# Batch 1 transposed on TensorE, and a work order planned anew with other transfer and clock costs

## The chip, the cores and the metric

The kernel runs on one core of one Trainium2 chip, in a single launch. The metric is the device time of a whole execution in microseconds. Every matrix product runs on TensorE (PE in the profile; its weight loads are PEld). VectorE is DVE, ScalarE is ACT, GpSimd is POOL. All transfers are issued by one queue, SyncE's (SP, SPq where its queue is meant), and carried by the core's 16 DMA engines.

## The reference

Eight batches of x (512 rows x 256) attend to a context (512 x 512 per batch), and then go through a mixture of 16 experts, of which each row uses 8, plus one shared expert. Cut to what matters:

```python
# attention
src_trans = (einsum('bsf,of->bso', ctx, W_src) + b_src) * mask      # keys and values
tgt_trans = (einsum('btf,of->bto', layernorm(x), W_tgt) + b_tgt) * mask
attn = softmax(where(mask == 0, -inf, q @ k / sqrt(32)))            # 8 heads of 32
x = x + concat(layernorm(x), attn @ v) @ W_out + b_out
# mixture of experts on layernorm(x)
scores = sigmoid(l2norm(xf) @ l2norm(gate_w).T)                     # 16 experts, top 8
routed = sum over experts of combine * ((silu(xf @ w_gate) * (xf @ w_up)) @ w_down)
x = x + routed + silu(xf @ sw_gate) * (xf @ sw_up) @ sw_down
```

## The kernel before

Each float32 operand of a product is split into two float16 halves, a high one and a low one, and each product is three TensorE matmuls (`mm3`: low by high, high by low, high by high). The split costs one ScalarE instruction for the high half and one subtract, on VectorE or GpSimd, for the low one.

A matmul sums over the partitions, so x, the attention output and the routed input have to be transposed. The kernel has two ways. For batch 0, TensorE multiplies by the identity into PSUM (tiles xT, oT, fT), and `split` reads PSUM: ScalarE writes the high half, VectorE the low one. For batches 1 to 7, `turn` splits the natural rows in SBUF first (tiles xm, om, fm of the pool `c16`), and two DMA transposes per `turn` bring 32 blocks each into xh, oh and f. In xm and om the low half is made by GpSimd, in fm by VectorE. The context goes the same way (cn to ch, 64 blocks a transfer), and so do the attention weights (pn to pt, 128 blocks a transfer, 128 of them in all).

Attention works in units: a batch has eight (two groups of four heads by four row blocks). A unit writes its scores s into the only score buffer (S=1, four PSUM banks), VectorE takes the row maximum nm, ScalarE scales it and computes four exponentials p. Two pairs of p are then rounded on ScalarE (pn high), subtracted on GpSimd (pn low, 128x1024), transposed by DMA into pt, and multiplied by v on TensorE (tile o). The scores of the next unit can only be written when the four p have read those before.

The experts (`ffn`) run over 17 weight sets in four groups, with the products g and u (up to 512 columns) and y. The weights arrive as float32 (tiles raw) during the setup, and are split on ScalarE and VectorE into w.

No engine order is written by hand. `record` lists operations, each with an engine, an assumed duration, and a virtual time `vt` to which a table RANK adds an offset by kind of operation and by batch (-1 setup, 0, 1, 7, and 2 for the batches between). `schedule` simulates engines and buffers, and picks among operations within AHEAD of the oldest pending virtual time the one that can start first, ties by virtual time. The resulting order is the order of the instructions; each engine keeps it and waits on semaphores. SLOTS gives the number of buffers of each pool: `row` holds q32, the float32 query between its product and its split (two per batch), and in the setup gw_n, the gate weights; `oc` holds a unit's output.

At run time, the planner's costs have no influence beyond the order and the buffer that they chose. In the trace every recorded instruction has the same line (L1071, the call in the last loop), so groups are told apart by their tile names.

Of the kernel before, what the change touches and what calls it, by code (L numbers as in the profile page):

```python
# [9 lines left out]
F32 = mybir.dt.float32  # L10
# [9 lines left out]
P = 128  # L20
# [11 lines left out]
    x=2, n2=5, cx=4, c16=2, ch=1, xh=1, f=2, qk=4, row=2, mb=1, mx=2, mt=1, p32=2, pn=2, pp=3, v3=2, oc=2, oh=2,  # L32
# [98 lines left out]
class Plan:  # L131
# [5 lines left out]
    def add(self, eng, dur, calls, port=False, size=0, after=()):  # L137
        outs, ins = [], list(after)
        for _, out, args, kw in calls:
            outs += [o for o in (*out, kw.get("accum_out")) if is_view(o)]  # L140
            ins += [a for a in (*args, *(v for k, v in kw.items() if k != "accum_out")) if is_view(a)]
        name = (outs[0] if isinstance(outs[0], Buf) else outs[0].buf).name
        tag = "".join(c for c in name if not c.isdigit()).strip("_") + eng
        vt = self.vt + RANK.get(tag, {}).get(STAGE.get(self.batch, 2), 0.0)
        op = Op(eng, dur, calls, outs, ins, vt, len(self.ops), port, size)
        op.tag = (self.batch, tag)
        self.ops.append(op)
        return op
# [31 lines left out]
    def dve(self, n, meth, out, *args, **kw):  # L180
        calls = [self.call("vector." + meth, out, *args, **kw)]
        self.add("DVE", 150 + 1.04 * n + 66 * (meth == "scalar_tensor_tensor" and any(is_view(a) for a in args[1:2])), calls, port=self.shared(calls))
# [11 lines left out]
    def dmat(self, tiles, out, in_):  # L194
        self.add("SP", max(1240.0, 16.4 * tiles), [self.call("sync.dma_start_transpose", out, in_)], size=4000 * tiles)

    def dma(self, size, out, in_):
        self.add("SP", 360.0, [self.call("sync.dma_start", out, in_)], size=size)


AHEAD = 1.366
RANK = {
    "aACT": {0: 0.1537, 1: 0.0033, 2: -0.4983, 7: 0.1955},
    "aDVE": {0: 0.0254, 1: 0.2498, 2: -0.2428},
    "aPOOL": {0: -0.0113, 1: 0.6968, 2: 0.5586, 7: 0.0013},
    "amaPE": {-1: 0.2806},
    "ambPE": {-1: 0.1166},
    "bobDVE": {-1: 0.5078},
    "bobSP": {-1: -0.2061},
    "bvbDVE": {-1: 0.105},  # L210
    "cTPE": {0: 0.5508},
    "cbSP": {0: 0.2177, 2: 0.7056, 7: 0.5622},
    "cdSP": {0: 0.0041, 1: -0.029, 2: 0.2104},
    "chACT": {0: -0.6068},
    "chDVE": {0: 0.2153},
    "chSP": {1: 0.0075, 2: -0.8976, 7: -1.0876},
    "cnACT": {1: -0.6307, 2: -0.7293, 7: -0.9914},
    "cnDVE": {1: 0.0087, 2: -0.0023, 7: 0.0346},
    "colsSP": {-1: -0.0672},
    "csBPE": {2: -0.1535, 7: -0.0124},  # L220
    "csTPE": {0: -0.1204, 1: -0.0287, 2: -1.2814, 7: -0.0309},
    "ctACT": {0: 0.864, 1: 0.1003, 2: 0.7227, 7: -0.1018},
    "cxPOOL": {0: 0.6459},
    "cxSP": {-1: 0.0735, 1: 0.0526, 2: -0.9286, 7: -0.0609},
    "fACT": {0: 0.0039},
    "fDVE": {0: 1.0851},
    "fSP": {1: 0.3396, 2: -0.0242, 7: 0.4824},
    "fTPE": {0: 0.3035},
    "fmACT": {1: 0.3782, 2: -0.0974, 7: -0.0187},
    "fmDVE": {2: 0.5311, 7: -0.0959},  # L230
    "fmPE": {-1: -0.1267},
    "fmaPE": {-1: 0.1564},
    "fmbPE": {-1: -0.4319},
    "gPE": {0: 0.1235, 1: 0.207, 2: 0.1559, 7: 0.6056},
    "gTPE": {0: 0.3676, 1: 0.5965, 2: -0.1162, 7: -0.0034},
    "gsqDVE": {-1: -0.4317},
    "gw_nDVE": {-1: -0.1543},
    "gw_nSP": {-1: -2.0117},
    "gwsACT": {-1: 0.0234},
    "gwsDVE": {-1: 0.6316},  # L240
    "hACT": {0: -0.6213, 1: 0.3291, 2: -0.1853, 7: -0.0131},
    "hDVE": {0: 0.1408, 1: 0.0071, 2: -0.2515, 7: -0.0144},
    "hPOOL": {0: -0.3695, 1: 0.2141, 2: -0.0944, 7: 0.3346},
    "junkACT": {1: -0.0113, 2: -0.018, 7: 0.0007},
    "kACT": {0: 0.3565, 1: -0.9183, 2: -0.1216},
    "kDVE": {0: 0.4038, 1: 0.1818, 2: -0.0333, 7: 0.0991},
    "kPE": {0: -0.2174, 1: -0.0614, 2: -0.0344, 7: -1.3012},
    "lgPE": {0: 0.2761, 1: -0.3919, 2: -0.2135, 7: 0.0154},
    "mbSP": {-1: -0.7576, 1: 0.96, 2: 0.035, 7: 0.1462},
    "mcolDVE": {-1: -0.5544},  # L250
    "mkSP": {-1: -0.0456},
    "mkTPE": {-1: -0.2494},
    "mrDVE": {0: 0.88, 1: 0.1094, 2: 0.5668},
    "mvDVE": {0: 0.3115, 1: 0.2223, 2: 0.1576, 7: -0.6709},
    "mwDVE": {1: -0.5933, 2: 0.5831, 7: -0.1328},
    "nmACT": {0: 0.3158, 1: -0.251, 2: -0.0551, 7: -0.0427},
    "nmDVE": {0: 0.0026, 1: 0.0593, 2: -0.1259, 7: -0.1155},
    "oPE": {0: 0.0273, 1: -0.0232, 2: 0.0553, 7: 0.0423},
    "oTPE": {0: 0.1833},
    "ocACT": {0: 0.1024, 1: 0.1925, 2: 0.2005, 7: 0.4061},  # L260
    "ocDVE": {0: 0.1704, 1: -0.1219, 2: -0.6326, 7: -0.0917},
    "ohACT": {0: 0.4072},
    "ohDVE": {0: -0.1733},
    "ohSP": {1: 0.1129, 2: -0.0398, 7: -0.3174},
    "omACT": {2: 0.2922, 7: 0.0002},
    "omPOOL": {1: -0.0603, 2: -0.0508, 7: 0.7467},
    "onPOOL": {0: 0.7499, 1: -0.853, 2: -0.1829, 7: -0.2491},
    "onesPOOL": {-1: -0.3119},
    "ooPE": {0: 0.4931, 1: -0.4365, 2: -0.6844, 7: -0.4352},
    "outSP": {0: 0.4027, 1: -0.3028, 2: 0.4122, 7: 0.4538},  # L270
    "pACT": {0: 0.0182, 1: -0.6748, 2: -0.0234},
    "pnACT": {0: 0.2152, 1: 0.2561, 2: 0.1906, 7: 0.0196},
    "pnPOOL": {0: 0.1635, 1: 0.0141, 2: 0.2234},
    "ptSP": {0: 0.4655, 1: -0.4384, 2: 0.1266, 7: 0.3368},
    "qACT": {0: 0.1257, 1: -0.3375, 2: -0.3996, 7: -0.129},
    "qDVE": {0: -0.2704, 1: -0.4202, 2: -0.5367, 7: -0.2649},
    "qPE": {0: -0.3731, 1: -0.0506, 2: -0.194, 7: -1.1345},
    "qPOOL": {0: -0.0185, 1: 0.126, 7: -0.8731},
    "rDVE": {0: -0.1233, 1: -0.1058, 2: 0.0001, 7: -0.3334},
    "rawSP": {-1: -0.1474},  # L280
    "rhPOOL": {0: -0.1646, 1: -0.4627, 2: 0.6826, 7: 0.2987},
    "riDVE": {0: -0.198, 1: 0.6361, 2: 0.1284, 7: -0.0834},
    "sPE": {1: 0.0314, 2: -0.3686, 7: -0.8384},
    "scACT": {0: -0.0831, 1: 0.4518, 2: -0.1934, 7: -0.1498},
    "scDVE": {0: 0.3459, 1: -0.1583, 2: 0.1869, 7: -0.186},
    "scPOOL": {0: -0.0709, 1: 0.1093, 2: -0.1766, 7: 0.0205},
    "smallDVE": {-1: 0.3026, 1: -0.1537, 2: -0.254, 7: -0.5587},
    "smallPOOL": {-1: -0.2347, 0: -0.1282, 1: -0.3163, 2: 0.0089, 7: 0.0576},
    "sqwACT": {-1: -0.5218},
    "sqwPOOL": {-1: -0.1816},  # L290
    "tDVE": {0: 0.0006, 1: -0.5031, 2: 0.36, 7: 0.0922},
    "uDVE": {0: 0.1229, 1: 0.634, 2: -0.239, 7: -0.259},
    "uPE": {0: -0.1486, 1: 0.6035, 2: 0.715},
    "vACT": {0: 0.2058, 1: 0.1873, 2: -0.0086, 7: 0.1161},
    "vDVE": {0: 0.3577, 1: 0.1322, 2: -0.9791, 7: -0.0565},
    "vPE": {0: 1.1408, 1: -1.3367, 2: -0.1245, 7: 0.2457},
    "vPOOL": {0: -0.0824, 1: -0.3013, 2: -0.4353, 7: 0.59},
    "veDVE": {0: 0.124, 1: -0.0703, 2: -0.0253, 7: -1.3962},
    "vfDVE": {0: 0.0546, 1: -0.7051, 2: 0.0069, 7: 0.2438},
    "wACT": {-1: -0.1553},  # L300
    "wDVE": {-1: -0.0168},
    "wmaPE": {-1: -0.2382},
    "wmbPE": {-1: -0.7302},
    "woACT": {-1: -0.6539},
    "woDVE": {-1: 0.1164},
    "woTPE": {-1: 0.5609},
    "wo_nSP": {-1: 0.2082},
    "wsACT": {-1: -0.3273},
    "wsDVE": {-1: -0.0925},
    "wsTPE": {-1: 0.9299},  # L310
    "ws_naSP": {-1: -0.9149},
    "ws_nbSP": {-1: 0.0231},
    "wtACT": {-1: 0.4585},
    "wtDVE": {-1: 0.4299},
    "wtTPE": {-1: -0.4778},
    "wt_nSP": {-1: 0.0823},
    "xDVE": {0: 0.124, 1: 0.2257, 2: -0.3319, 7: 0.1379},
    "xPOOL": {0: -0.0121, 1: 0.02, 2: 0.1123, 7: -0.199},
    "xSP": {0: 1.1008, 1: 0.0058, 2: 0.0641, 7: 0.353},
    "xTPE": {0: 0.4516},  # L320
    "xfACT": {0: -0.1806, 1: 0.1451, 2: -0.1422, 7: -0.437},
    "xhDVE": {0: 0.6081},
    "xhSP": {1: 0.2024, 2: -0.7682, 7: 0.2589},
    "xmACT": {1: 0.1813, 2: 0.1954},
    "xmPOOL": {1: -0.0234, 2: 0.0256, 7: 0.0077},
    "xnACT": {0: 0.0363, 1: -0.1228, 2: 0.2161, 7: -0.0338},
    "xnSP": {-1: -4.4201, 1: -0.3353, 2: -0.0611, 7: -0.0009},
    "xoPE": {0: -0.2204, 1: -0.0378, 2: -0.3262, 7: -0.1335},
    "yPE": {0: 0.3541, 2: 0.148, 7: 0.1762},
# [772 lines left out]
```

## Time and profile before

| quantity | value |
|---|---|
| median of 3 runs (lowest, highest) | 963.44 us (959.19, 963.85) |
| profiled execution, its own time | 962.42 us |
| its span, first to last instruction | 960.3 us |
| PE busy / DVE / ACT / POOL | 860.6 / 668.5 / 654.2 / 680.4 us |
| mean granted TensorE clock | 0.972 of full |
| transfers | 152.43 MB in 395,542 packets |
| PE busy in 0 to 300 us, in 300 to 860 us | 227.79 us, 537.46 us |

A busy share is time with an instruction of that engine running. "Idle before" a group names the operation that ended the wait. PEclk is the clock that TensorE was granted. A window line has the busy time of PE, PEld, DVE, ACT and POOL in that stretch, the granted clock, the mean share of the DMA engines and their rate.

### The profile page before, as it was taken

The numbers are of one execution on the slowest core, as the hardware profiler recorded it, in microseconds if no ns is written. First come the engines' busy times: TensorE is split into PE (matmuls) and PEld (weight loads), VectorE is DVE, ScalarE is ACT, GpSimd is POOL, SyncE is SP. The second block draws the span as 40 slices with busy tenths as digits, with TensorE's granted clock in tenths as the row PEclk, the third lists the DMA queues.
The fourth block names the chain that finished last, engine by engine and source line by source line (L and its number), as shares of the span: only waits on it lengthen the run. The fifth ranks groups of instructions, "written<-read, shape, count | busy, mean of one in ns | idle before, by whom it ended". The sixth has DMA issues, their size and how long they took to land.

```text
span 960.3 us, 21139 instructions
## 1 busy us (share of the span) xinstructions
PE 860.6 (90%) x8007; PEld 547.0 (57%) x8007; DVE 668.5 (70%) x1311; ACT 654.2 (68%) x1133; POOL 680.4 (71%) x830
## 2 busy tenths in 40 slices
PE   3874768989789998989999999989999999999997
PEld 2452446766555565636655556646555666565655
DVE  6666778855876677757785688757886687567554
ACT  3588887874877687757786587757787777534231
POOL 4577778876768787677858786787848976853432
PEclk9886999999889999999999999999999999999999
DMA  8868787798699967999599977998499968951411
GB/s 254 271 124 175 138 157 130 151 197 162 121 205 184 201 133 139 211 191 178 104 198 182 197 145 137 204 191 181 88 189 197 178 110 144 214 120 26 123 56 44
DMA packets 395542, 152.43 MB, mean 159 GB/s; under 512 B 347008, under 2 KB 375216, under 8 KB 395440
## 3 DMA queue, kind: packets, MB, share of 16 engines
q1 hardware_dynamic: 395440, 151.08, 77.9%
q8 instruction: 63, 1.03, 0.5%
q14 instruction: 39, 0.32, 0.2%
HBM read 61.12 MB, written 4.46 MB: 68 GB/s over the span
## 4 chain that ended last, share of the span: by engine, by line
PE 55%; DMA 12%; ACT 11%; DVE 8%; POOL 5%; issue 3%; SPq 1%; POOLq 0%; ACTq 0%; DVEq 0%
PE y L1071 14%; PE u L1071 13%; PE g L1071 12%; DMA pt<-pn 8%; PE s L1071 4%; ACT p L1071 3%; PE o L1071 3%; POOL pn L1071 3%; PE v L1071 3%; DVE nm L1071 3%; PE k L1071 2%; ACT pn L1071 2%; DMA cb<-cd 2%; PE oo L1071 2%; SPq L1071 1%
## 5 line engine op out<-in xcount | busy, mean ns | idle before, releaser
L1071 POOL TENSOR_TENSOR pn<-p,pn 128x1024 f16<-128x1024 f32 x128 | 274.6, 2151 | 57.8 <-ACT pn L1071 48.7
L1071 PEld LDWEIGHTS <-w 128*128 128x128 f16 x1836 | 172.1, 98 | 172.1 <-issue 19.3
L1071 POOL TENSOR_TENSOR a<-a,cb 128x512 f32<-128x512 f32 (+1 forms) x144 | 166.1, 1165 | 73.5 <-DVE a L1071 34.6
L1071 ACT ACTIVATE p<-s,nm,small 128x512 f32<-128x512 f32 x256 | 192.3, 782 | 10.6 <-POOL pn L1071 8.1
L1071 PE MATMUL g<-f,w 128*128 128x512 f16 (+1 forms) x918 | 194.7, 357 | 3.7 <-DVE oc L1071 1.3
L1071 PE MATMUL u<-f,w 128*128 128x512 f16 (+1 forms) x918 | 194.1, 358 | 1.6 <-DVE a L1071 1.6
L1071 PE MATMUL y<-w,h 128*128 128x256 f16 x1632 | 185.9, 273 | 5.6 <-DVE h L1071 4.1
L1071 PEld LDWEIGHTS <-h 128*128 128x128 f16 x1632 | 158.5, 98 | 32.0 <-DVE h L1071 6.7
L1071 ACT CAST pn<-p 128x1024 f16<-128x1024 f32 x128 | 134.5, 1053 | 60.8 <-DMA pt<-pn 60.7
L1071 DVE TENSOR_REDUCE nm<-s 128x4 f32<-128x2048 f32 x64 | 146.2, 2285 | 14.7 <-PE s L1071 14.6
L1071 ACT ACTIVATE a<-g,small 128x512 f32<-128x512 f32 (+1 forms) x153 | 98.1, 645 | 51.7 <-PE g L1071 49.8
L1071 DVE SCALAR_TENSOR_TENSOR a<-a,g 128x512 f32<-128x512 f32 (+1 forms) x153 | 94.5, 622 | 39.1 <-ACT a L1071 38.0
L1071 ACT CAST h<-u 128x512 f16<-128x512 f32 (+1 forms) x117 | 62.8, 540 | 51.0 <-DVE u L1071 49.2
L1071 PEld LDWEIGHTS <-pt 128*128 128x128 f16 x2048 | 69.8, 97 | 36.8 <-DMA pt<-pn 16.5
L1071 DVE TENSOR_TENSOR h<-u,h 128x512 f16<-128x512 f32 (+1 forms) x117 | 72.6, 625 | 25.7 <-ACT h L1071 24.1
L1071 DVE SCALAR_TENSOR_TENSOR x<-y,small,x 128x512 f32<-128x512 f32 x64 | 47.8, 748 | 60.9 <-PE y L1071 60.6
L1071 DVE TENSOR_TENSOR u<-u,a 128x512 f32<-128x512 f32 (+1 forms) x108 | 68.4, 635 | 27.5 <-PE u L1071 22.7
L1071 PE MATMUL o<-v,pt 128*128 128x65 f16 (+1 forms) x2048 | 74.2, 187 | 13.5 <-DMA pt<-pn 10.9
L1071 PE MATMUL s<-k,q 32*128 32x512 f16 x768 | 56.1, 396 | 21.2 <-ACT p L1071 20.7
L1071 POOL TENSOR_TENSOR on<-oc,r 128x128 f32<-128x128 f32 x64 | 30.1, 472 | 31.9 <-DVE oc L1071 20.1
L1071 POOL TENSOR_TENSOR h<-a,h 128x512 f16<-128x512 f32 (+1 forms) x36 | 40.3, 1120 | 15.2 <-ACT h L1071 14.9
L1071 PE MATMUL k<-ch,ws 128*128 128x512 f16 x192 | 45.6, 390 | 5.4 <-DMA ch<-cn 4.1
(188 smaller groups left out, 1055.8 us busy)
## 6 DMA issues: line engine op xcount, KB each, us to landing
cb<-cd SPq DMA_DIRECT2D x112, 256.0 KB, 3.9
cx<-in_ctx_dram SPq DMA_DIRECT2D x32, 256.0 KB, 3.6
xn<-in_x_dram SPq DMA_DIRECT2D x16, 256.0 KB, 3.4
x<-in_x_dram SPq DMA_DIRECT2D x8, 512.0 KB, 4.3
cb<-cd SPq DMA_DIRECT2D x32, 128.0 KB, 3.5
out_dram<-x SPq DMA_DIRECT2D x16, 256.0 KB, 3.1
mb<-in_mask_BxS_fk_dram SPq DMA_DIRECT2D x8, 256.0 KB, 4.6
raw<-in_L_ffn_w_gate_dram SPq DMA_DIRECT2D x16, 128.0 KB, 3.3
```

The lines of the kernel that those rows point to most:

```text
L1071: getattr(getattr(nc, eng), m)(*[real(v) for v in (*out, *args_)], **{k: real(v) for k, v in kw.items()})
```

## The change

Batch 1 joins batch 0 in the TensorE way: x, the attention output o and the routed input f ("second x") are transposed by TensorE and split out of PSUM. Batches 2 to 7 keep the DMA. The planner gets other costs: a longer VectorE duration for wide instructions on the port it shares with GpSimd, a lead time and a rate for transfers with a difference between transposes and plain ones, a time in which the SP queue is held by a running transpose, and a model of TensorE's clock. The table RANK and AHEAD are replaced, so the order of nearly all instructions can differ. `row` has one buffer where it had two, `oc` three where it had two. The short VectorE sequence that makes a power of two out of the context's largest row norm takes four instructions per batch where it took seven (one is added in the setup).

```diff
-    ... row=2, ... oc=2, oh=2,
+    ... row=1, ... oc=3, oh=2,
...
     def dve(self, n, meth, out, *args, **kw):
-        self.add("DVE", 150 + 1.04 * n + 66 * (...), calls, ...)
+        self.add("DVE", 150 + 1.04 * n + 280 * (self.shared(calls) and n > 500) + 66 * (...), calls, ...)
...
     def dmat(self, tiles, out, in_):
-        self.add("SP", max(1240.0, 16.4 * tiles), [...], size=4000 * tiles)
+        self.add("SP", max(1240.0, 16.4 * tiles), [...], size=4994 * tiles, lead=570.0 + 2.2 * tiles)
     def dma(self, size, out, in_):
-        self.add("SP", 360.0, [...], size=size)
+        self.add("SP", 430.0, [...], size=size)
...
-AHEAD = 1.366
+AHEAD = 1.59852454716
 RANK = {
...
-    "gw_nSP": {-1: -2.0117},
+    "gw_nSP": {-1: 0.4107},
...
+HALFWIN, COLD, HOT = 1706.5, 0.49, 0.82
+class Clock:
+    def __init__(self):
+        self.w, self.cold, self.n, self.busy, self.before = 0, False, 0, 0.0, HALFWIN
+    def run(self, t, work):
+        while True:
+            while self.w < int(t / HALFWIN):
+                f = (self.busy + self.before) / (2 * HALFWIN)
+                self.n += 1
+                if self.cold:
+                    self.cold = f <= HOT or self.n % 2 == 1
+                elif f < COLD:
+                    self.cold, self.n = True, 0
+                self.before, self.busy = self.busy, 0.0
+                self.w += 1
+            end, r = (self.w + 1) * HALFWIN, 2.0 if self.cold else 1.0
...
-        op.start, op.end = st, st + op.dur
+        op.start, op.end = st, clock.run(st, op.dur) if e == "PE" else st + op.dur
...
-            dma_free = max(dma_free, op.end + 900.0) + op.size / 250.0
+            dma_free = max(dma_free, st + op.lead) + op.size / 272.0 + 700.0 * (turned and op.lead == 950.0)
+            turned = op.lead < 950.0
             op.end = dma_free
+            if op.lead < 950.0:
+                free[e] = max(free[e], dma_free - 1250.0)
...
-    gsq = Buf("row", [P, D], F32, "gsq")
+    gsq = Buf("act", [P, D], F32, "gsq")
...
-        chain = [tt(f2[:, 0:1], f2[:, 0:1], cf2[:1], ALU.max),
-                 ts(ex[:, 0:1], ex[:, 0:1], 23, None, ALU.logical_shift_right), ...
+        chain = [stt(f2[:, 0:1], f2[:, 0:1], 2.0, cf2[:1], ALU.mult, ALU.max),
+                 ts(ex[:, 0:1], ex[:, 0:1], 24, 23, ALU.logical_shift_right, ALU.logical_shift_left), ...
...
-            if b == 0:
+            if b < 2:
                 t = ps(f"xT{b}{k}")
...
-            if b:
+            if b > 1:
                 turn(on, oh, 0, f"om{b}{hf}", p.pool)
...
-            if b:
+            if b > 1:
                 turn(xf, f, c, f"fm{b}{c}")
-        for k in range(0 if b else 2):
+        for k in range(0 if b > 1 else 2):
             t = ps(f"fT{i}{k}")
```

## The prediction

> **What bounds the kernel now.** I read the busy shares and slices of the page first, then busy time by stretches, then the waits of TensorE in each stretch, and last the timeline at the longest waits.
>
> ```profile
> span 960.3 us, 21139 instructions
> ...
> PE 860.6 (90%) x8007; PEld 547.0 (57%) x8007; DVE 668.5 (70%) x1311; ACT 654.2 (68%) x1133; POOL 680.4 (71%) x830
> ...
> PEclk9886999999889999999999999999999999999999
> ```
>
> PE is the only engine near its limit, and its clock is full except in the first 12 of 40 slices. The stretches (busy PE, PEld, DVE, ACT, POOL; clock; DMA share; GB/s) say where PE is not busy:
>
> ```profile
> 0.00:60.00 60.00, 38.65 (x300) 25.31 (x301) 36.29 (x108) 34.97 (x65) 34.89 (x60) 0.91 0.82 235
> 60.00:100.00 40.00, 21.89 (x279) 15.52 (x277) 26.84 (x57) 32.12 (x51) 28.66 (x35) 0.74 0.85 164
> 100.00:200.00 100.00, 81.69 (x964) 60.81 (x964) 82.81 (x181) 86.02 (x163) 82.70 (x117) 0.98 0.78 146
> 200.00:300.00 100.00, 85.56 (x857) 57.88 (x854) 61.69 (x134) 71.38 (x131) 71.10 (x98) 0.91 0.90 170
> 300.00:860.00 560.00, 537.46 (x4985) 327.90 (x4984) 403.94 (x737) 399.08 (x675) 427.12 (x477) 1.00 0.86 168
> 860.00:960.00 100.00, 95.37 (x632) 59.59 (x629) 56.93 (x99) 30.63 (x53) 35.94 (x46) 1.00 0.21 62
> ```
>
> PE idles 72.2 us in the first 300 (21.4, 18.1, 18.3 and 14.4), 22.5 in the next 560, and 4.6 at the end. Busy time times the missing clock, summed over 20 us windows, is another 18.4 us up to 300 (6.0 of it in 60 to 100, 4.7 in 260 to 280). So about 90 us could be had before 300, and 27 after, where the kernel is PE's. The waits of PE in 60 to 100, 200 to 300 and 300 to 860 (total, times, longest):
>
> ```profile
> PE s L1071 <- ACT p L1071: 14.0, 2, 7.0
> ```
> ```profile
> PE lg L1071 <- DMA f<-fm: 3.9, 3, 3.5
> PE k L1071 <- DMA ch<-cn: 2.9, 2, 2.5
> PE csB L1071 <- DVE small L1071: 2.8, 1, 2.8
> PE q L1071 <- DMA xh<-xm: 1.4, 1, 1.4
> ```
> ```profile
> PE o L1071 <- DMA pt<-pn: 10.3, 8, 3.1
> ```
>
> In 60 to 100 the score loop of batch 0 bounds: scores, maximum, exponentials, one buffer. In 200 to 300 it is transfers: the DMA share is 1.06 in 200 to 220 and 1.03 in 260 to 280. The PE timeline shows what a wait does to the next product:
>
> ```profile
> 100.78 0.83 PE L1071 MATMUL s<-k,q 32*128 32x512 f16 x12 [0.87 <-ACT p L1071]
> ...
> 89.27 1.47 PE L1071 MATMUL s<-k,q 32*128 32x512 f16 x12 [7.01 <-ACT p L1071]
> ```
> ```profile
> 212.79 4.45 PE L1071 MATMUL k<-ch,ws 128*128 128x512 f16 x12 [2.47 <-DMA ch<-cn]
> ...
> 223.87 2.75 PE L1071 MATMUL k<-ch,ws 128*128 128x512 f16 x12
> ```
>
> The same twelve matmuls take 1.47 against 0.83 us, and 4.45 against 2.75, when the clock was lowered.
>
> **The change part by part.** Sums are made against the profiled execution: 962.42 us, of which 960.3 are span and 2.1 lie around it. The median of the runs is 1.0 higher.
>
> *Transposes of batch 1.* Added: 24 TensorE transposes. Batch 0 has the same counts in the trace: xT 2.4 us of PE for eight, oT 1.2, fT 1.8, together 5.4. The x part falls near 97 us, where PE is busy 12.8 of 20 us; other waits hide it (without them 2.4 more). The o and f parts fall at 205 to 268, and I put their 3.0 on the path. Removed: twelve DMA transposes of 1.25 us of SP issue each (15 us; four in 99 to 106, eight in 213 to 265), so the attention transposes queued behind come up earlier. Six ScalarE casts of 0.62 become six of 0.59, no change. GpSimd loses four subtracts of 1.16 (4.6 us), VectorE gains four of 0.68 (2.7); fm's two on VectorE become two of f. VectorE is busy 82.8 of 100 us at worst, so the 2.7 lie beside PE. The lg wait of 3.9 goes; next in line is the split of f, for which batch 0's lg waited 0.8, so 3.1 are saved. Of the k and q waits on transfers (4.3) I take half, 2.1, since batch 2's cn and xm still go by DMA but stand behind fewer transfers. The six new PSUM tiles each hold one of four banks for a cast and a subtract, 1.3 us, which the waits of the batch 0 tiles (under 1 us each) make small. Ends: +3.0 if other waits take the place of these, -4.4 if all go. Taken: 3.0 - 3.1 - 2.1 = -2.2.
>
> *The price of a TensorE transpose.* By the rows above one costs 0.15 to 0.30 us of PE. The Trainium skill, VectorE: DVE Perf Modes, section The three transpose paths, gives 390 ns for a 128x128 bfloat16 block on TensorE and 1309 ns on the DMA. By its figure the 24 would be an estimated 9.4 us of PE, and the forecast 4 us later; the trace's durations (for float32) are used.
>
> *The score loop in 60 to 100.* Each round of 10.4 us has ScalarE idle while the maximum is made (3.39 us before nm at 83.17), and then puts a pn of 1.04, a w of 0.93 and two cn of 0.71 among the four p that free the scores. These 3.4 us per round would fit into the idle time. The old planner counts 16 x 61 ns = 0.98 us for the scores, the cold rows show 1.9 (1.47 and the mask rows), so it took the gap for shorter; the new one slows cold PE work by two. Two rounds give 6.8 at most from this, ScalarE's whole idle time there is 7.9. Taken -6.0. Ends: 0 (or +6 if the new order puts as much between the p of two more rounds), -14 with both waits gone. A gain here passes to the end, because batch 0's experts start after it and PE is full later on.
>
> *The clock.* The k row shows a lowered clock after a wait of only 2.47 us, so short waits cost too, and I count no separate gain: it is inside the ends. The Trainium skill, TensorE: Matmul & The Clock Gate, Part 1, says that the clock halves after an idle window of about 3.4 us. By that rule alone only the two 7 us waits and the 3.5 us one would cost clock, and I would add nothing for the rest; the 4.45 us row does not fit it.
>
> *The short VectorE chain.* Three instructions of 0.14 to 0.19 us fewer per batch, one more in the setup (0.15). PE waited for the chain three times in all. Three times 0.4, less 0.15: -1.0. Ends -1.5 and 0.
>
> *The rest of the order.* In 100 to 200 ScalarE is busy 86.0 of 100 and PE idles 18.3: 14 us is the most that a better order can give, and a worse one could lose as much as 10 (a further round of 10.4). Taken -3.0. In 300 to 860, 22.5 us of PE idle are left, of which 10.3 wait for pt; transfers priced nearer to the 4.7 us that pt takes to land should be asked for earlier. Taken -4.0; ends -10.3 and the loss of the second rival. In the setup (0 to 60) the first scores come at 39.9 after a line of loads and small steps; nothing that the diff shows shortens it, taken 0, ends -5 and +5. The last 100 us are PE's, taken 0.
>
> *One row buffer.* The second query product must now wait until GpSimd has read the first q32. In the trace the life of the first q32, from the end of its product to the end of GpSimd's subtract, is 2.8 to 8.9 us (batch 2: 230.5 to 233.3; batch 3: 418.8 to 427.7; three others 4.3 to 6.0), and in five batches of eight the two products stand back to back. What stands behind the waiting product on PE is everything. It is covered if three or four expert products of 1.3 us are put between; the order can do that, as the pair at 316.6 and 325.5 us has it already. Taken 0, ends 0 and 8 x 4 = 32. The gate weights gw_n lie in `row` too, from their load to the transposes at 39.3 to 39.6. Loaded first they would hold up the first query product (23.7) by up to 16 us; loaded after both q32 of batch 0 (the second is free at 37.7) they cost nothing, since logits need them only at 118.6. RANK moves their load from -2.01 to +0.41, so to later: taken 0, ends 0 and +16. The third oc buffer can only remove waits; PE waited 1.3 us once for oc. Zero.
>
> Sum: -2.2 - 6.0 - 1.0 - 3.0 - 4.0 = -16.2; 962.4 - 16.2 = 946.
>
> **The rivals.**
> *PE is the bound and the order gives nothing.* The early waits change place but not sum; 5.4 us of PE more, 3.1 of lg less: 963 to 965. For it: after 300 us PE is busy 96%. Against: the 14 us in 60 to 100 have a visible remedy.
> *Slower: the single q32 stalls PE.* From 2.0 us per batch (16.2 / 8) on, it eats the gain; at 4 us, near the middle of the lives seen, it costs 32 and ends at 978. For it: the life up to 8.9 us is set by GpSimd's queue, which is busy 71%. Against: the planner's durations for this chain (1.15 us for the subtract, 0.59 for the cast) are close to the rows (1.16, 0.62).
> *Slower: the steady stage loses its cover.* If each of seven batches waits once more for pt at the longest 3.1 us, and the first 100 us gain nothing, that is 22 - 6 = +16, 978 again. For it: the whole order is new; against: transfers are the thing now priced dearer.
> *Much faster.* The ends together, without the setup's, are about -44, so 918; half of what lies beyond the forecast gives 932 and lower.
>
> **How the numbers follow.** Forecast (933 to 957 as its own range) 0.50; much faster 0.13; nothing gained 0.11; q32 stall 0.13; steady stage worse 0.13. Faster by over 0.5% (4.8 us, about what a measurement here tells from no change) is 0.63, within it 0.11, slower 0.26. The range leaves out some 0.08 on each side: from 922, between the much faster case's middle and its end, to 980, just above both slower cases.
>
> **What would show it.** Right: the s waits on p in the first 110 us fall from 14 to about 8; lg of batch 1 waits for f's split and not for fm; pt waits of PE after 300 fall under 8 us; the clock in 60 to 100 is above 0.74; PE busy stays near 860 less what cold time goes. Wrong: a row "PE q <- POOL q" of over 16 us in total; the first scores of batch 2 (now at 233.9) later than before; PE idle in 300 to 860 above 30 us.

## The result: 1.3% slower

| | before | changed |
|---|---|---|
| median of 3 runs (lowest, highest), us | 963.44 (959.19, 963.85) | 974.57 (968.80, 979.48) |
| ratio, 95% interval | | 1.0133 [1.0092, 1.0175] |
| profiled execution / its span, us | 962.42 / 960.3 | 979.48 / 977.3 |
| PE busy / mean granted clock | 860.6 us / 0.972 | 878.7 us / 0.951 |

The profiled execution of the changed kernel is the slowest of its three, so the two traces are 17.0 us apart where the medians are 11.1 apart. I forecast 946 us.

The page of the changed kernel, head and clock by slices:

```profile
span 977.3 us, 21143 instructions
...
PE 878.7 (90%) x8031; PEld 560.2 (57%) x8031; DVE 679.4 (70%) x1292; ACT 653.9 (67%) x1133; POOL 671.1 (69%) x826
...
PEclk8866878999999999999999999999999999999999
```

PE idles 98.6 us (99.7 before) and is busy 18 us longer, of which the added transposes can be 5.4 at most: the rest is time at half clock. Twice the missing clock times the span is 95.8 us at half clock, against 53.8 before. It looks as if the clock were the loss. But the other two executions of the changed kernel had a clock of 0.961 (974.57 us) and 0.963 (968.80 us), and the 82 executions of the kernel before that were timed beside the experiments have 0.956 to 0.972, 0.964 in the mean, at a median of 961 us: at the same clock the changed kernel is still slower. The experiments below say the same. The stretches are those of the prediction:

```profile
0.00:60.00 60.00, 40.03 (x294) 27.67 (x295) 38.94 (x120) 32.48 (x61) 32.54 (x72) 0.85 0.72 216
60.00:100.00 40.00, 23.43 (x260) 14.80 (x259) 28.61 (x39) 31.88 (x49) 23.96 (x20) 0.63 0.83 158
100.00:200.00 100.00, 82.13 (x878) 58.18 (x876) 76.84 (x167) 81.39 (x155) 75.81 (x103) 0.86 0.71 140
200.00:300.00 100.00, 92.00 (x982) 65.35 (x981) 71.38 (x149) 78.13 (x148) 72.47 (x105) 0.97 0.86 169
300.00:860.00 560.00, 529.02 (x4856) 324.61 (x4855) 396.23 (x700) 392.60 (x660) 418.82 (x473) 0.99 0.82 164
```

Busy time times clock is the work done at full speed. In the four stretches up to 300 us it is 34.0, 14.8, 70.6 and 89.2 us, 208.6 in all; before it was 35.2, 16.2, 80.1 and 77.9, together 209.4. So the changed kernel loses 12 us up to 200 and has won 11 of them back at 300; its waits for transfers in 200 to 300 are 5.1 us, where they were 8.4. From 300 to 860 it is busy 8.4 us less, at a clock 0.01 lower: the loss of the profiled run arises there, and all of it after 460 us. The two parts of that stretch, first before, then changed:

```profile
300.00:460.00 160.00, 149.09 (x1388) 90.24 (x1390) 112.24 (x207) 115.72 (x196) 124.24 (x134) 1.00 0.92 177
460.00:860.00 400.00, 388.38 (x3601) 237.66 (x3594) 291.69 (x531) 283.36 (x481) 302.88 (x344) 1.00 0.84 164
```
```profile
300.00:460.00 160.00, 151.13 (x1355) 91.63 (x1354) 114.49 (x197) 116.22 (x196) 126.14 (x134) 0.99 0.89 178
460.00:860.00 400.00, 377.89 (x3503) 232.98 (x3502) 281.73 (x503) 276.38 (x464) 292.68 (x340) 0.99 0.79 158
```

Multiplied instruction by instruction, busy time times clock is 149.1 us before and 149.4 changed in the first part, 386.8 and 373.4 in the second. By the same finer sum the first 300 us lose 3 us and not 1. That early balance is rough: four profiles of the new order up to there (of the changed kernel, and of late_from_before, p_first and after_halves, explained below) range from 207 to 215 us. In 460 to 860 three profiles of the new order have 373 to 375 us (changed, p_first, after_halves) and three of the old one 386 to 387 (before, before_halves, turns_alone).

The waits of TensorE in 300 to 860 (total, times, longest; all rows from 1.8 us on):

```profile
PE o L1110 <- DMA pt<-pn: 6.6, 5, 2.4
PE s L1110 <- ACT p L1110: 5.9, 6, 2.2
PE g L1110 <- DVE h L1110: 3.8, 5, 1.6
PE g L1110 <- DVE sc L1110: 2.2, 1, 2.2
PE lg L1110 <- DMA f<-fm: 2.0, 4, 0.9
PE xo L1110 <- DVE v L1110: 1.8, 1, 1.8
```

The pt waits are down from 10.3 to 6.6 us, but only up to 460 us (4.5 to 0.7); after that they are 5.8 and 5.9, and in the first 300 us they are up from 0.6 to 11.3. Over the whole span they have grown, before and changed:

```profile
PE o L1071 <- DMA pt<-pn: 10.9, 10, 3.1
```
```profile
PE o L1110 <- DMA pt<-pn: 17.9, 12, 2.6
```

And p now holds up the scores of batches 3, 5 and 6, which it never did after 300 us before, and VectorE ends many small waits. Summed over all rows of this view by what ended the wait, in 300 to 860 us, for kernels of this study, and the sum and the full-speed work of TensorE in 460 to 860 alone (us):

| kernel | DMA | DVE | ACT | all, GpSimd too | all, after 460 | work after 460 | ratio to before |
|---|---|---|---|---|---|---|---|
| before | 12.6 | 8.7 | 0 | 22.1 | 11.2 | 386.8 | 1 |
| changed | 9.2 | 14.9 | 6.5 | 30.6 | 21.9 | 373.4 | 1.0133 |
| late_from_before | 9.9 | 12.0 | 1.7 | 24.2 | 15.7 | 381.0 | 1.0058 |
| late_from_after | 13.3 | 16.7 | 4.5 | 34.5 | 25.2 | 367.9 | 1.0206 |
| p_first | 9.1 | 18.3 | 4.7 | 32.4 | 20.4 | 374.1 | 1.0158 |
| after_halves | 13.2 | 8.7 | 3.6 | 25.5 | 17.2 | 375.1 | 1.0202 |
| turns_alone | 12.6 | 6.8 | 0 | 19.9 | 12.0 | 386.1 | 0.9979 |
| turns_swapped | 10.3 | 6.6 | 0 | 16.9 | 8.7 | 391.0 | 0.9954 |

Of the 10.7 us of waits that the changed kernel has more after 460 us, 5.2 end with VectorE (3.5 to 8.7), 5.3 with ScalarE (0 to 5.3) and 1.0 with a transfer (6.9 to 7.9); waits for GpSimd are 0.8 us fewer.

### The profile page after: what moved, and what is told of

Its sections match the earlier page's. It is cut to its first block, busy times and chain, and to the rows that moved or that the text cites. A ratio compares the mean times of both kernels' runs of the same rounds, so it can differ in the third digit from the quotient of the medians.

```text
span 977.3 us, 21143 instructions
## 1 busy us (share of the span) xinstructions
PE 878.7 (90%) x8031; PEld 560.2 (57%) x8031; DVE 679.4 (70%) x1292; ACT 653.9 (67%) x1133; POOL 671.1 (69%) x826
## 4 chain that ended last, share of the span: by engine, by line
PE 44%; DMA 4%; DVE 4%; ACT 3%; POOL 2%; issue 1%; SPq 0%; POOLq 0%; DVEq 0%; ACTq 0%
PE y L1110 13%; PE u L1110 11%; PE g L1110 9%; PE s L1110 2%; DMA pt<-pn 2%; PE o L1110 2%; PE k L1110 2%; PE v L1110 2%; PE oo L1110 1%; ACT p L1110 1%; POOL pn L1110 1%; PE q L1110 1%; DVE nm L1110 1%; PE xo L1110 1%; DMA cx<-in_ctx_dram 1%
## 5 line engine op out<-in xcount | busy, mean ns | idle before, releaser
L1110 PEld LDWEIGHTS <-w 128*128 128x128 f16 x1836 | 175.7, 99 | 178.2 <-issue 27.8
L1110 POOL TENSOR_TENSOR a<-a,cb 128x512 f32<-128x512 f32 (+1 forms) x144 | 169.9, 1190 | 57.0 <-DVE a L1110 34.5
L1110 PE MATMUL g<-f,w 128*128 128x512 f16 (+1 forms) x918 | 198.9, 362 | 9.1 <-DVE h L1110 4.3
L1110 PE MATMUL u<-f,w 128*128 128x512 f16 (+1 forms) x918 | 196.4, 358 | 2.5 <-DVE a L1110 1.7
L1110 PE MATMUL o<-v,pt 128*128 128x65 f16 (+1 forms) x2048 | 76.5, 188 | 19.5 <-DMA pt<-pn 17.9
L1110 ACT ACTIVATE nm<-nm,small 128x4 f32<-128x4 f32 x64 | 24.8, 387 | 43.6 <-DVE nm L1110 43.4
L1110 POOL TENSOR_TENSOR h<-a,h 128x512 f16<-128x512 f32 (+1 forms) x36 | 38.2, 1060 | 21.7 <-ACT h L1110 21.6
```

The source lines that it names most:

```text
L1110: getattr(getattr(nc, eng), m)(*[real(v) for v in (*out, *args_)], **{k: real(v) for k, v in kw.items()})
```

## The experiments

For those that keep or join orders, `schedule` is replaced by a written list, in this form; the operations are recorded as in the kernel named.

```diff
+ORDER = """ ... """   # numbers of the operations, in the order of the list
+SLOT = """ ... """    # the buffer of each tile, in order of first use
 def schedule(ops):
-    ...
+    by = {o.seq: o for o in ops}
+    slot = iter(SLOT.split())
+    r = [by[int(n)] for n in ORDER.split()]
+    for o in r:
+        for b in o.bufs:
+            if b.pool in SLOTS and b.slot is None:
+                b.slot = int(next(slot))
+    return r
```

**Transposes alone** (`turns_alone`): the list of the kernel before, with the edit

```diff
-            if b == 0:
+            if b < 2:
                 t = ps(f"xT{b}{k}")
```

and the same for o and f, the table, costs and buffers as before.

> The list of the kernel before, every common operation in its old place and its old order on its engine; only batch 1's x, o and f are transposed by TensorE, with the new transposes, casts and subtracts put where the halves for the DMA were made. My prediction's term for this was -2.2 us (ends -4.4 and +3.0). Theory A, the transposes pay as priced: 958 to 963 us against 963.4, and batch 1's wait of lg for the transferred f (3.9 us) is gone. Theory B, the transposes are what made the changed kernel slower: 966 us or more. Theory C, they bring more than I priced because the queue of transfers gets shorter (the changed kernel regained 9 us between 200 and 300 us): 955 us or less.

Measured: 960.41 us, ratio 0.9979 [0.9956, 1.0003], so -2.0 us (-4.2 to +0.3, which just includes no change). Theory A. Its waits in 200 to 300 us have no row of lg for a transferred f; k waits 2.4 us, where it waited 2.9:

```profile
PE s L1224 <- ACT p L1224: 4.8, 4, 1.6
PE k L1224 <- DMA ch<-cn: 2.4, 2, 1.6
```

The transposes did not make the kernel slower. Everything that did is in the order, or in what the order was made for.

**Half of each order** (`late_from_before`, `late_from_after`): the edit is the list alone.

> The list of the changed kernel up to the operations that started before 460 us in its profile; everything later in the order of the list before. The operations are those of the changed kernel. At 460 us the changed kernel was 2.8 us of TensorE work behind the one before, at the end 16.7 us. Theory A, the order of the steady stage costs the other 14 us: 960 to 966 us. Theory B, the loss comes from the state that the first 460 us leave behind (buffers, the queue of transfers) and any order would lose it: 972 to 979 us. The seam itself may cost 1 to 3 us.

> The counterpart of late_from_before: the operations and the list of the kernel before for all that started before 260 us in its profile (batch 1 transposed by DMA), everything later in the order of the changed kernel, with its one row buffer not used. late_from_before left a loss of 4.6 us of the changed kernel's 14 to 15. Theory A, the steady order costs 10 to 14 us wherever it stands: 971 to 977 us. Theory B, the new order is good as long as it starts from its own beginning, or the loss comes from the changed setup: 960 to 965 us.

Measured: 966.79 us, 1.0058 [1.0037, 1.0079]; and 981.58 us, 1.0206 [1.0186, 1.0226]. Both lie above the range of their theory A, by 0.8 and 4.6 us. With the old order from 460 us on, the changed kernel gets back some 7 of its 13 us by these ratios. With the new order from 260 us on, the kernel before loses 20, more than the whole change does, although its first 260 us and both row buffers are kept. So the loss comes with the steady order, whatever stands ahead of it, and theory B of the second run (it needs its own beginning, or the setup is at fault) falls. The seam may have its part in the 20. The stretch 460 to 860 of the two:

```profile
460.00:860.00 400.00, 384.44 (x3537) 234.53 (x3538) 285.62 (x511) 279.07 (x473) 298.70 (x341) 0.99 0.82 162
```
```profile
460.00:860.00 400.00, 374.65 (x3445) 229.28 (x3444) 285.19 (x509) 277.35 (x464) 288.03 (x337) 0.98 0.79 157
```

`late_from_before` also shows what the new setup costs: with the changed kernel's list up to there, its full-speed work up to 300 us (38.38 x 0.91, 24.05 x 0.66, 80.47 x 0.91, 92.09 x 0.98) is 214 us, 5 more than the kernel before. The late first scores (50.71 us in the changed kernel against 39.90) are paid back by 300, as far as the spread of 207 to 215 us lets one say.

**The clock** (`after_kept_warm`, `before_kept_warm`):

```diff
     for op in ops:
+        if op.seq in WARM:
+            bank, n = WARM[op.seq]
+            ...
+            for _ in range(n):
+                nc.tensor.matmul(t, tiles["sel"].tile, tiles["ws"].tile[:, 0, 0, :], start=True, stop=True)
```

> The changed kernel, its list untouched, and in 17 places where TensorE waited 0.8 us or more, ahead of the waiting product, 2 to 11 matmuls (79 in all, 17 us at full clock) into a PSUM bank that is free there; nothing reads their result. The computation is unchanged. Theory A, the time at half clock (98 us against 56) is itself the loss of 14 to 17 us: with TensorE kept busy the clock stays up, and the kernel ends at 960 to 968 us, with under 50 us at half clock. Theory B, other engines set the pace where the clock is low and a faster TensorE would only wait longer: 972 to 979 us whatever the clock does. Theory C, the added matmuls overshoot the waits: slower than 980.

> The same with the kernel before: in 19 places 2 to 18 matmuls (106 in all, 23 us at full clock) whose result nothing reads, its list untouched. Time at half clock was 56 us, worth about 20 us of TensorE work after 40 us. Theory A, the lost clock is lost time: 950 to 957 us. Theory B, the low clock lies beside waits for other engines: 961 to 965 us. Theory C, overshoot: above 966.

Measured: 977.58 us, 1.0164 [1.0137, 1.0190], mean clock 0.968 (62 us at half clock); and 960.50 us, 0.9981 [0.9962, 1.0000], clock 0.980 (38 us). The clock came up as meant, about a third of the cold time went, and the time stayed. So theory B for the changed kernel; for the one before some 2 us are in it. A rival is that the added matmuls ran past the waits and ate the gain. In the kernel before they hardly did: in its trace only 2 of 19 fillings run straight into the waiting product, for under 1 us in all. In the changed kernel 8 of 17 do, for at most 5 us in all; less these 5 it would be at 972 to 973 us, still outside theory A. So the half clock lies mostly where TensorE would else wait: in 60 to 100 us, where the clock is lowest, the score loop sets the pace. `turns_warm` joined the filling with the transposes:

> turns_alone with matmuls whose result nothing reads in 20 places where its TensorE waited 0.8 us or more (90 in all, 20 us at full clock). Each of the two alone measured 0.998 of the kernel before. Theory A, they add up: 957 to 959 us, 0.995 to 0.997. Theory B, they remove the same waits: 960 to 961 us.

Measured: 961.40 us, 1.0007 [0.9992, 1.0023]. The two do not add up: theory B.

**One row buffer** (`one_row_buffer`), in the list of the kernel before:

```diff
-    ... qk=4, row=2, mb=1, ...
+    ... qk=4, row=1, mb=1, ...
...
-    gw_n = Buf("row", [P, S], F32, "gw_n")[:E, :D]
+    gw_n = fixed("gw_n", [P, D])[:E]
```

> The list of the kernel before with one row buffer where it had two (gw_n gets a place of its own, so that only the two q32 of a batch share the buffer); in five batches the second query product now has to stand behind the first q32's subtract, with what was behind it in the list. My prediction gave this 0 us with ends 0 and 32. Theory A, a planned order covers it but an order that was not planned for it pays the life of q32 (2.8 to 8.9 us) in five to eight batches: 975 to 995 us. Theory B, expert products slip in front and cover it: 962 to 968 us.

Measured: 971.82 us, 1.0099 [1.0073, 1.0125], +9.5 us: between the theories. The wait sits on VectorE, which writes q32, and not on TensorE:

```profile
DVE q L1223 <- POOL q L1223: 11.1, 4, 4.6
```

The changed kernel has no such row, because its order keeps the two query products of each batch 4.8 to 18 us apart (of batch 4 at 423.6 and 432.5 us; before at 417.4 and 418.7). In an order made for it, one buffer costs no wait of its own; it does take freedom from the order.

**What holds TensorE up in the steady stage** (`p_first`, `after_halves`). Two waits of the changed kernel, with the engine that ended them. ScalarE ahead of the scores at 560.95, where four other instructions stand between the last p of the unit and those before it:

```profile
556.24 1.46 ACT L1110 ACTIVATE p<-s,nm,small 128x512 f32<-128x512 f32 x2
557.58 0.60 ACT L1110 CAST h<-u 128x512 f16<-128x512 f32 x1
558.04 1.08 ACT L1110 CAST pn<-p 128x1024 f16<-128x1024 f32 x1
558.99 0.72 ACT L1110 ACTIVATE k<-k,small 128x512 f16<-128x512 f32 x1
559.57 0.64 ACT L1110 CAST om<-on 128x512 f16<-128x512 f32 x1
560.08 0.82 ACT L1110 ACTIVATE p<-s,nm,small 128x512 f32<-128x512 f32 x1
```
```profile
560.95 1.47 PE L1110 MATMUL s<-k,q 32*128 32x512 f16 x12 [2.25 <-ACT p L1110]
```

And VectorE ahead of xo at 625.19: a ve of 128x4, which takes 0.16 us elsewhere, takes 2.08 and ends with GpSimd's pn, and v stands behind it (VectorE, GpSimd, TensorE):

```profile
622.46 2.08 DVE L1110 TENSOR_SCALAR ve<-mv 128x4 f32<-128x4 f32 x1
624.46 0.68 DVE L1110 TENSOR_TENSOR v<-v,v 128x512 f16<-128x512 f32 x1
```
```profile
621.95 2.57 POOL L1110 TENSOR_TENSOR pn<-p,pn 128x1024 f16<-128x1024 f32 x1
```
```profile
625.19 1.47 PE L1110 MATMUL xo<-wo,xh 128*128 128x256 f16 x12 [1.81 <-DVE v L1110]
```

The first was tried by moving p in the list, the second by

```diff
-                    p.pool(1024, "tensor_tensor", pn[:, 1], pf, pn[:, 0], ALU.subtract)
+                    p.add("POOL", 130 + 2.0 * 1024, [p.call("gpsimd.tensor_tensor", pn[:, 1, h_], pf[:, h_], pn[:, 0, h_], ALU.subtract) for h_ in (slice(0, S), slice(S, 2 * S))], port=True)
```

> The changed kernel with 51 of the exponentials p of batches 4 to 6 moved ahead on ScalarE by up to 2 us, in front of casts and other work that the new order put between the p of one unit; every other engine keeps its order. In the changed kernel TensorE waits 5.3 us for ScalarE in 480 to 760 us, in the kernel before 0. Theory A, the new order on ScalarE cuts the score units too fine, and that wait is what starts the cold stretches: 967 to 973 us. Theory B, ScalarE and VectorE have no slack there, so what is moved back makes others late: 975 to 983 us.

> The changed kernel with its list untouched; each of GpSimd's 128 subtracts pn (128x1024, 2.13 us) is issued as two of 128x512, so that GpSimd lets go of the port it shares with VectorE about every 1.1 us. In the changed kernel VectorE's instructions took 42.9 us longer in all than the same instructions at their short duration, in the kernel before 31.9 (fm 1.3 to 2.7 us where the short one is 0.68, cn up to 2.7 where it is 0.75). Theory A, the new order leaves VectorE no room for these stalls and TensorE waits for what stands behind them: VectorE's excess falls to about 25 us and the time to 966 to 972 us. Theory B, the stalls are beside the point, GpSimd only gets 128 more fixed costs (some 12 us beside 671): 976 to 983 us.

> The same in the kernel before, list untouched. Its TensorE waits for VectorE only 8 us after 300 us, against 15 in the changed kernel. Theory A: VectorE's excess falls from 32 to about 20 us, the time by 1 to 4 us: 957 to 961. Theory B: 961 to 966 us.

Measured: p_first 977.63 us, 1.0158 [1.0135, 1.0180]; after_halves 981.48, 1.0202 [1.0173, 1.0230]; before_halves 965.33, 1.0030 [1.0009, 1.0051]. Theory B each time: what was aimed at went down and the time did not. p_first: waits for ScalarE from 6.5 to 4.7 us in 300 to 860, for VectorE from 14.9 to 18.3. after_halves: VectorE's excess over short durations from 42.9 to 35.7 us (32 to 29 in the kernel before), waits for VectorE from 14.9 to 8.7 and for ScalarE from 6.5 to 3.6, but for transfers from 9.2 to 13.2 (pt alone from 6.6 to 10.7); that pt comes later because GpSimd's work got longer is likely, but was not followed up. The sum of waits fell by 5.1 us there and the clock of the stretch from 0.99 to 0.98. So neither of the two waits alone is the cause: where one was shortened, other waits or time at half clock took its place.

One explanation would be that the new order leaves less room ahead of TensorE. That room can be measured in the traces: for each product, the time from the end of the last VectorE, ScalarE or GpSimd instruction that it reads, or whose bank it takes over, to its own start.

| kernel | 300 to 460 us: median, under 0.3 us | 460 to 860 us: median, under 0.3 us |
|---|---|---|
| before | 2.65 us, 10 of 116 | 2.05 us, 33 of 305 |
| changed | 1.59 us, 24 of 115 | 2.08 us, 44 of 293 |
| late_from_after | 1.55 us, 22 of 117 | 2.23 us, 35 of 290 |
| turns_swapped | 2.64 us, 3 of 116 | 1.80 us, 42 of 307 |

It does not fit. The room is much smaller in 300 to 460 us, where the changed kernel loses nothing, and nearly the same after 460 us, where it loses 13; there late_from_after, which loses most, has the most room of the four, and turns_swapped, the fastest in the table of waits, the least. Single instructions that come 2 us late (ve above) do stall TensorE. But what in the new order makes it wait longer for VectorE and ScalarE after 460 us stays open, and which of the planner's new prices led there was not tried.

**A faster version** (`turns_swapped`, `turns_swapped_2`): `turns_alone` with the list changed where TensorE waited.

> turns_alone with four pairs changed in TensorE's order, at the four longest waits after 300 us (2.4, 1.2, 1.6 and 2.8 us, all for a transferred pt): the product after the waiting one, whose inputs were there, goes in front. Theory A, a wait of TensorE in the steady stage is lost whole, with the clock behind it: 8 us of waits shrink to 2, 953 to 956 us. Theory B, the wait comes back at the next place: 959 to 961 us.

> turns_swapped with seven more products put in front of a product that waited 0.7 to 1.9 us in its profile (three o in 102 to 133 us, one g at 270, three u at 311, 422 and 691), 8 us of waits in all. Theory A, such waits are lost whole: 952 to 955 us. Theory B, in the first 300 us the score loop sets the pace and the later ones come back elsewhere: 956 to 959 us.

Measured: 957.05 us, 0.9954 [0.9932, 0.9976]; and 954.88 us, 0.9944 [0.9921, 0.9967]. Four exchanged pairs bring some 2.5 us beyond `turns_alone`, though the intervals of the two overlap; the time lies between the theories. The row of pt falls from 10.0 to 5.8 us over the whole span.

```profile
PE o L1224 <- DMA pt<-pn: 10.0, 8, 2.8
```
```profile
PE o L1224 <- DMA pt<-pn: 5.8, 8, 1.9
```

The second time lies in the range of theory A, but the two kernels were timed in different sessions, and by the ratios, whose intervals overlap, the seven more exchanges cannot be told from the four. Both are faster than the kernel before and than the changed one. In the changed kernel the same rule found a product to put in front at only two of its 18 waits of over 0.6 us after 300: elsewhere the products behind needed a bank that was still taken or inputs that were not there.

## Why the prediction was wrong

**Transposes of batch 1, -2.2: right, as far as the interval of -4.2 to +0.3 goes.** Alone they gave -2.0, lg of the changed kernel waited for f's split (1.3 us in 200 to 300), and the k and q waits fell only in part, as I took them.

**The score loop, -6.0: the wait went, the gain did not.** The waits of s for p in the first 110 us fell from 15.7 to 9.6 us, close to the 8 I named, and in 60 to 100 from 14.0 to 9.6. But the clock there is 0.63 and not above 0.74, and pt (3.7 us) and the weights' fm (1.6) hold TensorE up in the same 40 us: full-speed work is 14.8 us against 16.2. "A gain here passes to the end" failed with it.

**Setup, 0; gw_n, 0 because "loaded later".** The second step was wrong: I read the table's offset as a time. gw_n was loaded at 10.9 us, held the one buffer until its transposes at 39.78, and the first query product came right behind them, at 40.00 where it had been at 23.7 us. That is the 16 us of my upper end, as a delay of q; the scores came 10.8 us later. But v and k of batch 0 were put in its place, and by 300 us at most 3 us of it are left. The price of 0 was right, for another reason.

**The rest of the order, 100 to 200, -3.0: +9.5 us** by full-speed work, at my end of +10; with the 11 us won in 200 to 300 it is one shift of work over the border. Up to 300 us I had counted -12 in all; the profile shows 1 to 3 lost, `late_from_before` 5 won.

**The steady stage, -4.0: this step failed, and with it the sign.** "Transfers priced nearer to the 4.7 us that pt takes to land should be asked for earlier" was to take 4 of the 10.3 us of pt waits after 300. They fell by 3.7 us, but as a shift: all of it before 460 us, with 10.7 us more of them in the first 300. And the sum had no term for waits for other engines, though the whole order was new: after 460 us the waits for VectorE and ScalarE went from 3.5 to 14.0 us, and the time at half clock from 3.4 to 10.2. TensorE's full-speed work there is 13.4 us less (386.8 to 373.4), of the 17 us between the two profiled executions; the two exchanged lists show that it is the order that costs this. My rival of this place ("the steady stage loses its cover", 978) had the place and nearly the time, but through more pt waits, which is not what happened there: that it came near is luck. "PE idle in 300 to 860 above 30 us" was the sign I had named for it, and it reads 31.0.

**One row buffer, 0: right for this order** (no row of q waiting for q, and the first scores of batch 2 at 232.9, not later than 233.9), and one_row_buffer put a price on it in an order that was not made for it: 9.5 us, of ends 0 to 32. (The life of 418.8 to 427.7 us that I gave to batch 3 is batch 4's; the sum does not change.)

**The clock, no gain of its own: right as a gain,** since the cold stretches lie mostly beside waits; that new waits after 460 us could lower it further had no term. The short VectorE chain (-1.0) was not told apart.

## What to carry to other kernels

Judge an order searched against a cost model by all waits of the full engine, stage by stage, and not by the one wait that it was to remove: here the pt waits fell in one stage, rose in another, and waits for two other engines came up in a third. Where several engines are 67 to 70% busy around one that is full, a wait taken away can come back as the next in line, as in three runs here: take the removed wait as the upper end, and look for what stands 1 us behind it. A small repair at measured waits (four exchanged pairs, 0.46% below the old time with the transposes) did better than a whole new plan. And an explanation that fits the kernel in question (less room ahead of TensorE) has to be held against the other runs, faster and slower, before it is believed.

## What the runs showed of the hardware

*Short waits and the clock.* A wait of 2.25 us in the steady stage is followed by a cold product; the second row is the same 48 matmuls in the kernel before.

```profile
705.09 0.85 PE L1110 MATMUL o<-v,pt 128*128 128x65 f16 x16 [2.25 <-DMA pt<-pn]
705.77 7.91 PE L1110 MATMUL y<-w,h 128*128 128x256 f16 x48
```
```profile
699.54 5.40 PE L1071 MATMUL y<-w,h 128*128 128x256 f16 x48
```

So around a wait of 2.25 us the loss was 4.8: the wait, and 2.5 us more for the product. The Trainium skill, TensorE: Matmul & The Clock Gate, Part 1, has the clock fall after an idle window of about 3.4 us; this wait is shorter, and the measurement decides. Not every such wait does it: in the kernel before, the clock stayed at 1.00 after waits of 2.95 us (ending at 375.19) and 3.06 us (at 423.19). What decides between them was not looked into. And the filled waits show the other half: raising the mean clock from 0.951 to 0.968 in the changed kernel, and from 0.972 to 0.980 in the one before, was worth nothing in the first and some 2 us in the second.

*A tiny instruction blocked for the whole of another.* The ve of 0.16 us that took 2.08 ended within 0.02 us of GpSimd's pn. This agrees with the Trainium skill, SBUF — State Buffer, section SBUF: two separate sides, which says of the ports that VectorE and GpSimd share that whichever starts first has them for its whole instruction while the other is fully blocked. The page names which VectorE instructions use these ports; no run here shows whether ve is one of them. Cutting GpSimd's instruction in two took a sixth off VectorE's excess in the changed kernel, not the two fifths that I had expected.
